# One-layer attention and expert block on one core: fewer rotation-table loads, a later start of the second chunk's projections, one idle product less

## The chip, the cores and the metric

The kernel runs on one core of a Trainium2 chip. The engines of the core that matter here are TensorE (PE in the profile: matrix products, with its weight loads shown apart as PEld), VectorE (DVE), ScalarE (ACT), GpSimd (POOL), and SyncE (SP), which does nothing but issue DMA transfers. ACT and POOL issue some transfers too. The metric is the time of one execution on the device in microseconds (us); of several executions the median is taken.

## The reference

The input x has 2048 rows of 256 numbers. The block is latent attention with rotated positions, then a layer norm, then an expert network, then a second layer norm:

```python
q = (x @ Wq).reshape(B, S, 16, 16)            # 16 heads of 16
c_kv = x @ Wkv_down                           # 64 latent columns
k = (c_kv @ Wk_up)...;  v = (c_kv @ Wv_up)...
q_rope, k_rope = rotated(last 12 of each head, cos, sin)
scores = where(causal, -inf, qf @ kf.T * 0.25)
x = layernorm(x + softmax(scores) @ v)
w, i = top_2_of(softmax(x @ gate_w.T))        # of 16 experts
x = layernorm(x + sum_e w_e * swiglu_e(x) + swiglu_shared(x))
```

All of it is in float32.

## The kernel before, in words

**Chunks, heads, steps.** The 2048 rows are worked on in four chunks `c` of 512. The 16 heads are four groups `g` of four; within a group each head takes 32 partitions: 0 to 15 for its numbers, 16 for a constant, and 20 to 31 for its 12 rotated numbers once more. For each group and chunk of queries the kernel first finds the largest score of each row (`Maxima`: products into four PSUM banks, one a head, then a DVE reduction of each, L515, or L509 on the diagonal, where the mask is added) and later the weighted values (`Weighted`: products, exponentials on ACT, values). Both are cut into steps, listed in `steps`. The dictionary `at` says what else is done at the end of a step: `prologue(c)` turns chunk c of x on PE (eight transposes, tile `pt`, copied to `xT`) and computes its latent columns (tile `pc`, copied to `ckv`); `project_k`, `project_q` and `project_v` compute a group's keys, queries and values of one chunk.

**Order.** PE executes strictly in the order of the program (L142 to L149). All products write to eight PSUM banks taken in turn, so a product waits until the reader of the bank's last content is done. The other engines have their own queues, in an order that the framework chooses.

**The start.** L750 to L756: three idle products (`warm`, 128x512, each two passes on PE as all float32 products are) on constants, then `prologue(0)`, `project_k(0, 0)`, `project_q(0, 0)` and `prologue(1)`. Then come the steps. Steps 0, 1 and 2 are the three diagonal maxima of group 0, chunk 0; steps 3 to 6 the maxima of chunk 1's queries against chunk 0's keys; at step 7 the first weighted products join. `project_k(0, 1)` and `project_q(0, 1)` stand at the end of step 1, `prologue(2)` at the end of step 3, `project_v(0, 0)` at step 4, `project_k(0, 2)` at step 6, `prologue(3)` at step 7.

**Rotation.** `project_k` multiplies the keys' two products `pk` by a cosine and a sine table, `cs[c]` (128 partitions x 2 x 512), and adds the two. For group 0, chunk 0 both multiplications are DVE's (L430, L434); otherwise the second is copied by ACT (L436) and multiplied by POOL (L437). The sum is always POOL's (L439). `project_q` does the same with one table `cq[c]` (128 x 512), on DVE for group 0, chunk 0 (L450), else ACT and POOL (L452, L453). In each 32 partitions of `cs` and `cq` the first 20 come from rows 0 to 19 of the table in DRAM (`rope`, 32 rows x 2 x 2048, rows 17 to 31 zero) and the last 12 from rows 4 to 15: two loads for each of four heads, so eight loads for `cs[c]` and eight for `cq[c]` (`load_rope`, L317 to L326).

**Loads.** SP issues, in this order: chunk 0 of x (L350), `cs[0]`, chunk 1 of x, the value weights `wvs` twice (L361), the tables of chunk 1, chunk 2 of x, its tables, chunk 3 and its tables, the weights of the other groups, the gate, the experts' weights, and a clearing of a buffer in DRAM. ACT's queue issues the latent weights `wkds` (two loads), the key weights `wks[0]` (two loads, one for each 64 partitions), the query weights and `cq[0]`. All of these transfers share eight semaphores: each issue waits until the last transfer of its semaphore has landed. `double(g)` (L339) copies columns of the weights on POOL; it waits for their loads.

Of the kernel before, what the change touches and what calls it, by code (L numbers as in the profile page):

```python
# [13 lines left out]
ALU = mybir.AluOpType  # L14
# [3 lines left out]
P = 128  # L18
S, E = 2048, 256
H, HD, LAT = 16, 16, 64  # L20
NOPE, RD = 4, 12
G = 4
PAD = 32
LOW = HD + NOPE
ONE = HD
CH = 512
# [11 lines left out]


NBLK = 28  # L40
WARM = 3
LAST = 2
OFTEN, SELDOM = 9, 12
DEPTH = 2
# [6 lines left out]
def block_kernel(  # L51
# [14 lines left out]
    nc = tc.nc  # L66
# [8 lines left out]
        out=qmask, in_=qmask, pattern=[[-1, CH]], base=CH - P, channel_multiplier=1,  # L75
# [16 lines left out]
    cs = [const.tile([P, 2, CH], F32, tag=f"cs{c}", name=f"cs{c}") for c in range(3)]  # L92
# [15 lines left out]
        out=before, in_=before, pattern=[[1, P]], base=0, channel_multiplier=-1,  # L108
# [36 lines left out]
    def matmul(*args, **kw):  # L145
        pe(nc.tensor.matmul, *args, **kw)

    def transpose(*args):
        pe(nc.tensor.transpose, *args)  # L149
# [139 lines left out]
    with ExitStack() as att:  # L289
# [11 lines left out]
        wks = [ap1.tile([P, P], F32, tag=f"wks{g}", name=f"wks{g}") for g in range(G)]  # L301
        wvs = ap1.tile([P, G * P], F32, tag="wvs", name="wvs")
# [6 lines left out]
        cq = [ap1.tile([P, CH], F32, tag=f"cq{c}", name=f"cq{c}") for c in range(NCH)]  # L309
        ckv = [ap1.tile([2 * LAT, CH], F32, tag=f"ckv{c}", name=f"ckv{c}") for c in range(NCH)]  # L310
# [4 lines left out]
            )  # L315

        def load_rope(c, queries, queue):  # L317
            of = rope[:, :, c * CH : (c + 1) * CH]
            for j in range(4):
                r = PAD * j  # L320
                if queries:
                    queue.dma_start(out=cq[c][r : r + LOW], in_=of[:LOW, 0, :])
                    queue.dma_start(out=cq[c][r + LOW : r + PAD], in_=of[NOPE:HD, 1, :])
                else:
                    queue.dma_start(out=cs[c][r : r + LOW], in_=of[:LOW])
                    queue.dma_start(out=cs[c][r + LOW : r + PAD], in_=of[NOPE:HD])  # L326

        sines = {}

        def load_weights(g, queue):  # L330

            of = slice(g * P, (g + 1) * P)
            for a in range(2):
                queue.dma_start(out=wks[g][a * LAT : (a + 1) * LAT], in_=wk[:LAT, a, of])
            sines[g] = wkp.tile([P, 2, P], F32, tag="pr", name=f"sines{g}")
            for a, to in enumerate((wqs[g], sines[g])):
                queue.dma_start(out=to, in_=wq[:, a, of].rearrange("(k p) m -> p k m", p=P))

        def double(g):  # L339


            w = wks[g].rearrange("p (h d) -> p h d", d=PAD)
            nc.gpsimd.tensor_copy(w[:, :, LOW:], w[:, :, NOPE:HD])
            for k in range(2):
                w, o = (
                    a[:, k].rearrange("p (h d) -> p h d", d=PAD) for a in (wqs[g], sines[g])
                )
                nc.gpsimd.tensor_copy(w[:, :, LOW:], o[:, :, NOPE:HD])

        load_x(0)  # L350
        for a in range(2):
            nc.scalar.dma_start(
                out=wkds[:, :, a * LAT : (a + 1) * LAT], in_=wkd.rearrange("(k p) l -> p k l", p=P)
            )
        load_weights(0, nc.scalar)
        load_rope(0, False, nc.sync)
        load_x(1)
        load_rope(0, True, nc.scalar)
        double(0)
        for a in range(2):  # L360
            nc.sync.dma_start(out=wvs[a * LAT : (a + 1) * LAT], in_=wv[:LAT])  # L361
        load_rope(1, False, nc.sync)
        load_rope(1, True, nc.sync)
        load_x(2)
# [5 lines left out]
        for g in range(1, G):  # L370
            load_weights(g, nc.sync)
        nc.sync.dma_start(out=gw, in_=gate.rearrange("(k p) n -> p k n", p=P))
        for k in range(2):
            for w, at, o, n in (
# [3 lines left out]
                    out=w13[:, k, :, at : at + n],  # L378
                    in_=w[k * P : (k + 1) * P, :NF].rearrange("p (n f) -> p n f", f=INTER)[
                        :, :, o : o + n  # L380
                    ],
# [11 lines left out]
        for e in range(NEXP):  # L393
            nc.sync.dma_start(
                out=xg[e * S : (e + 1) * S, :].rearrange("(r p) e -> p r e", p=P),
                in_=blank.unsqueeze(1).to_broadcast([P, TT, ROW]),
            )
        nc.sync.dma_start(
            out=xg[NEXP * S :, :], in_=blank
        )  # L400

        qs, ks, vs, qa, pm, avs = {}, {}, {}, {}, {}, {}

        def bank(name):
            return ps_sc.tile([P, CH], F32, tag="sc", name=name)

        def prologue(c):

            copy = nc.scalar.copy if c else nc.vector.tensor_copy
            for k in range(2):  # L410
                pt = bank(f"pt{c}_{k}")
                for t in range(4):
                    transpose(pt[:, t * P : (t + 1) * P], xr[c][:, t, k * P : (k + 1) * P], ident)
                copy(xT[c][:, k, :], pt)
            pc = bank(f"pc{c}")
            for k in range(2):
                matmul(
                    pc, lhsT=wkds[:, k, :], rhs=xT[c][:, k, :], start=(k == 0), stop=(k == 1)
                )
            copy(ckv[c], pc)  # L420

        def project_k(g, c):
            tmp = wk1.tile([P, 2, CH], F32, tag="rot", name=f"rot{g}_{c}")
            pk = [bank(f"pk{g}_{c}_{a}") for a in range(2)]
            for a in range(2):
                r = slice(a * LAT, (a + 1) * LAT)
                matmul(
                    pk[a], lhsT=wks[g][r], rhs=ckv[c][r], start=True, stop=True
                )
            nc.vector.scalar_tensor_tensor(  # L430
                tmp[:, 0, :], pk[0], unit, cs[c][:, 0, :], ALU.add, ALU.mult
            )
            if (g, c) == (0, 0):
                nc.vector.tensor_tensor(tmp[:, 1, :], pk[1], cs[c][:, 1, :], ALU.mult)  # L434
            else:
                nc.scalar.copy(tmp[:, 1, :], pk[1])  # L436
                nc.gpsimd.tensor_tensor(tmp[:, 1, :], tmp[:, 1, :], cs[c][:, 1, :], ALU.mult)  # L437
            ks[g, c] = kv.tile([P, CH], F32, tag="k", name=f"k{g}_{c}")
            nc.gpsimd.tensor_tensor(ks[g, c], tmp[:, 0, :], tmp[:, 1, :], ALU.add)  # L439

        def project_q(g, c):
            pq = bank(f"pq{g}_{c}")
            for k in range(2):
                matmul(
                    pq, lhsT=wqs[g][:, k], rhs=xT[c][:, k, :],
                    start=(k == 0), stop=(k == 1),
                )
            qs[g, c] = wk3.tile([P, CH], F32, tag="q", name=f"q{g}_{c}")
            if (g, c) == (0, 0):
                nc.vector.tensor_tensor(qs[g, c], pq, cq[c], ALU.mult)  # L450
            else:
                nc.scalar.copy(qs[g, c], pq)  # L452
                nc.gpsimd.tensor_tensor(qs[g, c], qs[g, c], cq[c], ALU.mult)  # L453
# [184 lines left out]
        def whole_m(g, c):  # L638
            return [(g, c, t, kc) for t in range(4) for kc in range(c)]
# [31 lines left out]
        m = whole_m(1, 3)  # L671
# [5 lines left out]
        for g in range(1, G):  # L677
# [9 lines left out]
            else:  # L687
                m = whole_m(g + 1, 3)
# [22 lines left out]
        def put(step, what, *args):  # L711
            at.setdefault(step, []).append(lambda: what(*args))

        for step, what, c in (
            (1, project_k, 1), (1, project_q, 1), (3, prologue, 2), (4, project_v, 0),
            (6, project_k, 2), (7, prologue, 3), (9, project_v, 1), (9, project_q, 2),
            (14, project_k, 3), (17, project_q, 3), (19, project_v, 2), (32, project_v, 3),
        ):
            if what is prologue:
                put(step, what, c)  # L720
            else:
                put(step, what, 0, c)
# [27 lines left out]
        warm = bank("warm")  # L750
        for i in range(WARM):
            matmul(warm, lhsT=ones, rhs=qmask, start=True, stop=True)
        prologue(0)
        project_k(0, 0)
        project_q(0, 0)
        prologue(1)  # L756
        prior = None
        step = 0
        while step < len(steps) or prior or at:
            m, s = steps[step] if step < len(steps) else (None, None)  # L760
            m = m and Maxima(*m)
# [31 lines left out]
    for j, r, o in ((0, 0, slice(0, H1)), (1, 0, slice(H1, INTER)), (1, H2, slice(0, H1 - H2))):  # L793
        nc.sync.dma_start(
            out=w2r[r : r + o.stop - o.start, j],
            in_=w2[:NF, :].rearrange("(n q) e -> q n e", q=INTER)[o],
        )
    hidden_rows = [fp1.tile([P, 2, 2 * P], F32, tag=f"hT{i}", name=f"hT{i}") for i in range(3)]
    for a in hidden_rows:
# [16 lines left out]
        out=upto, in_=upto, pattern=[[1, NEXP], [-1, NEXP]], base=0, channel_multiplier=0,  # L816
# [404 lines left out]
```

## Time and profile before

| what | value |
| --- | --- |
| median of 11 executions | 779.58 us (776.95 to 780.95) |
| the profiled execution, its own time | 777.5 us |
| its span from first to last instruction | 775.8 us |
| mean granted clock of TensorE | 0.973 |
| instructions | 14499 |
| DMA | 72.55 MB, mean 94 GB/s |

Three views of the profile are used. The page gives each engine's busy time and share of the span, and the chain of work that ended last: followed back from the last instruction, at each step to whatever released it. The timeline lists groups of instructions with start, length, engine, line, output and inputs, shapes and count; in brackets stands how long the engine had been idle and what ended that. An engine name with a q at its end (SPq, ACTq) is the engine's sequencer, which issues DMAs. The windows give, for a stretch of time, the busy time and count of PE, PEld, DVE, ACT and POOL, then the clock that was granted to TensorE as a share of full speed, the busy share of the DMA engines and their rate.

The clock column shows 1.00 also where there is no record, as in the first microseconds.

### The profile page before, as it was taken

How to read it: one execution, taken by the hardware profiler on the slowest of the kernel's cores; microseconds unless marked ns; L12 is line 12 of the kernel's file. 1: busy time of each engine (PE TensorE's matmuls, PEld its weight loads, DVE VectorE, ACT ScalarE, POOL GpSimd, SP SyncE). 2: the span in 40 equal slices, each digit the busy share in tenths (PEclk: the TensorE clock that was granted, in tenths of full speed). 3: DMA queues.
4: the chain of work that ended last, by engine and by line, in shares of the span. 5: the costliest groups of instructions: out<-in, count | busy, mean ns of one | idle time of the engine just before them, and what ended most of it. 6: DMA issues, size and time to landing. Idle time of an engine off the chain costs nothing.

```text
span 775.8 us, 14499 instructions
## 1 busy us (share of the span) xinstructions
PE 733.4 (95%) x5074; PEld 361.5 (47%) x5074; DVE 524.7 (68%) x1434; ACT 445.0 (57%) x908; POOL 342.0 (44%) x510
## 2 busy tenths in 40 slices
PE   6898999999999999999999999999869989999994
PEld 3343443444334343544334444344234658887542
DVE  2677798887677887778688678897546623332275
ACT  1243647478787787777788778866443112223356
POOL 3241646534467455657454655440725304445300
PEclk9899999999999999999999999999969989999998
DMA  5459999992000000001000000000208233332172
GB/s 150 132 146 258 328 330 327 330 329 87 3 1 1 1 2 1 2 20 38 1 2 2 1 3 1 1 2 1 89 22 213 69 103 108 112 104 65 29 231 98
DMA packets 75981, 72.55 MB, mean 94 GB/s; under 512 B 20890, under 2 KB 70141, under 8 KB 75904
## 3 DMA queue, kind: packets, MB, share of 16 engines
q1 hardware_dynamic: 70936, 62.43, 28.4%
q0 software_dynamic: 3504, 8.43, 3.2%
q10 hardware_dynamic: 1464, 0.72, 0.4%
q8 instruction: 42, 0.69, 0.4%
q14 instruction: 35, 0.29, 0.1%
HBM read 27.09 MB, written 45.65 MB: 94 GB/s over the span
## 4 chain that ended last, share of the span: by engine, by line
PE 80%; DVE 6%; issue 3%; DMA 3%; SPq 2%; ACT 2%; another core or an unknown queue 2%; POOL 1%; ACTq 0%; POOLq 0%; DVEq 0%
PE s L143 22%; PE av L143 17%; PE m L143 14%; PE py L143 4%; PE ab L143 4%; PE pq L143 3%; PE c L143 2%; PE pk L143 2%; PE ph L143 2%; PE pv L143 1%; PE px L143 1%; PE pz L143 1%; DVE pm L515 1%; PE lg L143 1%
## 5 line engine op out<-in xcount | busy, mean ns | idle before, releaser
L571 ACT ACTIVATE p<-s 128x512 f32<-128x512 f32 (+1 forms) x576 | 284.9, 580 | 106.4 <-PE m L143 62.4
L143 PE MATMUL m<-k,q 32*128 32x512 f32 (+3 forms) x1280 | 283.6, 566 | 4.7 <-POOL q L453 4.7
L143 PE MATMUL s<-qa,k 32*128 32x512 f32 (+3 forms) x1280 | 275.7, 560 | 3.6 <-DVE qa L533 2.0
L515 DVE TENSOR_REDUCE pm<-m 128x1 f32<-128x512 f32 x384 | 237.6, 684 | 46.1 <-PE m L143 45.0
L610 POOL TENSOR_TENSOR avs<-avs,more 128x512 f32<-128x512 f32 (+2 forms) x110 | 128.7, 1170 | 129.4 <-ACT more L609 118.8
L143 PEld LDWEIGHTS s<-qa,k 32*128 32x128 f32 x1280 | 110.0, 187 | 118.0 <-ACT p L571 58.6
L143 PE MATMUL av<-p,v 128*32 128x512 f32 (+3 forms) x1280 | 150.5, 546 | 0.6 <-ACT p L571 0.5
L509 DVE CUSTOM_DVE_ANT_0 m<-m,qmask 128x128 f32<-128x128 f32 (+3 forms) x256 | 117.6, 526 | 40.1 <-PE m L143 33.4
L143 PEld LDWEIGHTS m<-k,q 32*128 32x128 f32 x1280 | 112.3, 184 | 35.2 <-issue 9.6
L143 PEld LDWEIGHTS av<-p,v 128*32 128x32 f32 x1280 | 28.1, 108 | 99.5 <-ACT p L571 56.6
L982 POOL DMA_INDIRECT yg<-yb,to x41 | 40.4, 984 | 74.0 <-ACT yb L970 53.1
L580 POOL TENSOR_SCALAR_AFFINE_SELECT p<-p 128x128 f32<-128x128 f32 (+1 forms) x192 | 59.6, 330 | 28.7 <-ACT p L571 26.9
L609 ACT COPY more<-av 128x512 f32<-128x512 f32 (+2 forms) x110 | 60.8, 553 | 19.9 <-PE av L143 14.8
L143 PE MATMUL h<-xT,cs 128*128 128x512 f32 (+1 forms) x96 | 43.3, 597 | 2.3 <-ACT u L836 1.4
L281 POOL DMA_INDIRECT xg<-xr,slot x32 | 31.2, 975 | 21.4 <-issue 15.7
L143 PE MATMUL py<-w2r,hT 112*128 112x256 f32 (+1 forms) x164 | 39.8, 380 | 0.0
L509 DVE DVE_READ_ACCUMULATOR2_ANT pm<- 128x1 f32 x256 | 36.7, 143 | 0.0
L143 PE MATMUL ab<-xT,w 128*112 128x256 f32 x128 | 33.9, 388 | 0.0
L143 PEld LDWEIGHTS py<-w2r,hT 112*128 112x128 f32 x164 | 30.8, 190 | 6.1 <-ACT hT L1021 0.5
L143 PE MATMUL pq<-xT,wqs 128*128 128x512 f32 x64 | 31.7, 618 | 0.0
L437 POOL TENSOR_TENSOR rot<-rot,cs 128x512 f32<-128x512 f32 x15 | 19.1, 1270 | 23.9 <-ACT rot L436 23.9
L143 PEld LDWEIGHTS h<-xT,cs 128*128 128x128 f32 (+1 forms) x96 | 16.9, 181 | 24.1 <-issue 17.4
(166 smaller groups left out, 658.1 us busy)
## 6 DMA issues: line engine op xcount, KB each, us to landing
xg<-hot SPq DMA_DIRECT2D x16, 2064.0 KB
xb<-xg SPq DMA_DIRECT2D x16, 258.0 KB
got<-yg SPq DMA_DIRECT2D x8, 512.0 KB
w<-in_w_dram SPq DMA_DIRECT2D x4, 896.0 KB
xr<-in_x_dram SPq DMA_DIRECT2D x4, 512.0 KB
w<-in_w_dram SPq DMA_DIRECT2D x4, 512.0 KB
out_dram<-o SPq DMA_DIRECT2D x8, 256.0 KB
w2r<-in_w_dram SPq DMA_DIRECT2D x1, 1792.0 KB
```

What stands on the lines that cost most here:

```text
L143: tc.keep_in_program_order(op(*args, **kw))
L281: put = nc.gpsimd.indirect_dma_start(out=xg[:, :], out_offset=bass.IndirectOffsetOnAxis(ap=slot[:, j, i : i + 1], axis=0), in_=xr[c][:, t, ...
L437: nc.gpsimd.tensor_tensor(tmp[:, 1, :], tmp[:, 1, :], cs[c][:, 1, :], ALU.mult)
L509: nc.vector.tensor_tensor_reduce(out=ps[:, of], in0=ps[:, of], in1=qmask[:, CH - (of.stop - of.start) :], scale=1.0, scalar=3.0 * NEG, op0 ...
L515: nc.vector.tensor_reduce(to, ps, AX.X, ALU.max)
L571: nc.scalar.activation(pr[:, :n], ps[:, :n], AF.Exp, scale=SCALE)
L580: nc.gpsimd.affine_select(out=diag, in_=diag, pattern=pattern, base=0, channel_multiplier=-1, compare_op=ALU.is_ge, fill=0.0,)
L609: nc.scalar.copy(more[:, n0:], pv[:, n0:])
L610: nc.gpsimd.tensor_tensor(to, to, more[:, n0:], ALU.add)
L982: nc.gpsimd.indirect_dma_start(out=yg[:, :], out_offset=bass.IndirectOffsetOnAxis(ap=to, axis=0), in_=yb, in_offset=None, bounds_check=2 * ...
```

## The change

The rotation tables in DRAM are used by their first 16 rows alone: 32 partitions are filled by rows 0 to 15 twice. A chunk's key table takes two loads (cosines, sines; 128 partitions, the 16 rows read eight times by a source step of zero) and its query table four (one a head: 16 cosine rows, then 16 sine rows). Two pairs of weight loads become one each. The warm products are two. The first keys' sum goes to DVE. `prologue` is split into `columns` (turning) and `latent`; only chunk 1's `columns` comes ahead of the steps, while its `latent`, `project_k` and `project_q` come at the end of step 0; chunk 2's prologue comes one step earlier, at the end of step 2.

```diff
-WARM = 3
+WARM = 2
...
         def load_rope(c, queries, queue):
-            of = rope[:, :, c * CH : (c + 1) * CH]
-            for j in range(4):
-                r = PAD * j
-                if queries:
-                    queue.dma_start(out=cq[c][r : r + LOW], in_=of[:LOW, 0, :])
-                    queue.dma_start(out=cq[c][r + LOW : r + PAD], in_=of[NOPE:HD, 1, :])
-                else:
-                    queue.dma_start(out=cs[c][r : r + LOW], in_=of[:LOW])
-                    queue.dma_start(out=cs[c][r + LOW : r + PAD], in_=of[NOPE:HD])
+            of = rope[:HD, :, c * CH : (c + 1) * CH]
+            if queries:
+                for j in range(4):
+                    queue.dma_start(
+                        out=cq[c][PAD * j : PAD * (j + 1)], in_=of.rearrange("d a n -> a d n")
+                    )
+            else:
+                for a in range(2):
+                    half = of[:, a].unsqueeze(0)
+                    queue.dma_start(out=cs[c][:, a], in_=half.to_broadcast([8, HD, CH]))
...
-            for a in range(2):
-                queue.dma_start(out=wks[g][a * LAT : (a + 1) * LAT], in_=wk[:LAT, a, of])
+            queue.dma_start(out=wks[g], in_=wk[:LAT, :, of].rearrange("l a m -> a l m"))
...
-        for a in range(2):
-            nc.sync.dma_start(out=wvs[a * LAT : (a + 1) * LAT], in_=wv[:LAT])
+        nc.sync.dma_start(
+            out=wvs, in_=wv[:LAT].unsqueeze(0).to_broadcast([2, LAT, G * P])
+        )
...
-        def prologue(c):
-
-            copy = nc.scalar.copy if c else nc.vector.tensor_copy
+        def mover(c):
+
+            return nc.scalar.copy if c else nc.vector.tensor_copy
+
+        def columns(c):
+
+            copy = mover(c)
             for k in range(2):
...
+        def latent(c):
             pc = bank(f"pc{c}")
...
-            copy(ckv[c], pc)
+            mover(c)(ckv[c], pc)
+
+        def prologue(c):
+            columns(c)
+            latent(c)
...
-            nc.gpsimd.tensor_tensor(ks[g, c], tmp[:, 0, :], tmp[:, 1, :], ALU.add)
+            adder = nc.gpsimd if g or c else nc.vector
+            adder.tensor_tensor(ks[g, c], tmp[:, 0, :], tmp[:, 1, :], ALU.add)
...
-            (1, project_k, 1), (1, project_q, 1), (3, prologue, 2), (4, project_v, 0),
+            (0, latent, 1), (0, project_k, 1), (0, project_q, 1), (2, prologue, 2),
+            (4, project_v, 0),
             (6, project_k, 2), (7, prologue, 3), (9, project_v, 1), (9, project_q, 2),
...
-        prologue(1)
+        columns(1)
```

More of the change, by code (lines that the diff above doesn't have):

```diff
@@ L718, in block_kernel @@
         ):
-            if what is prologue:
+            if what in (prologue, latent):
                 put(step, what, c)
```

## The prediction

> **What bounds the kernel now.** I read the page first, for the engines and the chain of work that ended last.
>
> ```profile
> PE 733.4 (95%) x5074; PEld 361.5 (47%) x5074; DVE 524.7 (68%) x1434; ACT 445.0 (57%) x908; POOL 342.0 (44%) x510
> ...
> PE 80%; DVE 6%; issue 3%; DMA 3%; SPq 2%; ACT 2%; another core or an unknown queue 2%; POOL 1%; ACTq 0%; POOLq 0%; DVEq 0%
> ```
>
> TensorE (PE) is busy 95% of the span and makes 80% of the chain. Work taken from another engine in mid-kernel would give nothing; but the DMA and SP shares of the chain (5%) must sit where PE has nothing to do, and all three edits lie in the first 45 us. So I went to the timeline of that stretch (start, length, engine, line; in brackets the engine's idle time and what ended it).
>
> ```profile
> 2.88 4.53 PE L143 MATMUL warm<-qmask,ones 128*128 128x512 f32 x6 [2.88 <-POOL ones L112]
> ...
> 12.09 0.51 SPq L313 DMA_DIRECT2D xr<-in_x_dram  x1
> ...
> 14.14 0.75 DVE L430 SCALAR_TENSOR_TENSOR rot<-pk,unit,cs 128x512 f32<-128x512 f32 x1 [2.80 <-DMA cs<-in_rope_dram]
> ...
> 16.40 1.88 PE L143 MATMUL pt<-ident,xr 128*128 128x128 f32 x8 [1.92 <-DMA xr<-in_x_dram]
> ...
> 18.10 2.89 PE L143 MATMUL pc<-xT,wkds 128*128 128x512 f32 x4
> ...
> 20.91 1.79 PE L143 MATMUL m<-k,q 32*128 32x512 f32 x16
> ...
> 30.13 2.08 PE L143 MATMUL m<-k,q 32*128 32x512 f32 x8 [2.69 <-POOL q L453]
> ...
> 37.00 2.48 DVE L515 TENSOR_REDUCE pm<-m 128x1 f32<-128x512 f32 x4 [2.31 <-PE m L143]
> ```
>
> Three stalls stand here. DVE waits 2.80 us for the first rotation table (14.14). PE waits 1.92 us for the second chunk of x (16.40), which SP issued only at 12.09, behind eight table loads. And though the first queries were ready at 16.08 and the first keys at 16.84, the first maxima wait until 20.91, because PE runs in program order and chunk 1's turning and latent product stand ahead. A fourth follows: q of chunk 1 comes late (PE idle 2.69 us to 30.13). From 37 us DVE is nearly always busy, until the rotation of chunk 2's keys at 44.78, my last mark. The windows give clock and DMA load (after the engines: granted clock, DMA share, GB/s).
>
> ```profile
> 14.00:16.00 2.00, 0.48 (x2) 0.00 (x0) 1.86 (x3) 0.00 (x0) 0.43 (x1) 1.00 0.99 334
> ...
> 17.00:19.00 2.00, 2.00 (x7) 1.38 (x7) 0.00 (x0) 1.17 (x2) 0.00 (x0) 0.50 0.28 81
> ```
>
> After the 1.9 us gap the clock is halved, so the work ahead of the first maxima is slow as well. And the DMA engines moved 334 GB/s where a large load was queued, 72 to 130 elsewhere before 30 us: the loads are bound by their issues and waits, not by bytes.
>
> **The change, part by part.** I lay the first 38 us out anew from measured lengths; times after the change are in italics.
>
> *Warm products.* One idle product less is two passes. Passes start 0.85 us apart (weight loads at 3.89, 4.74, 5.59). x's first chunk is there at 5.32, when SP's wait for it ends. The turning so starts at *6.3*, not 7.24: 0.9 us. Everything to the first queries' products follows at its old distances: latent product *7.7*, ckv *9.8* to *10.4* on DVE, keys' products *10.5*, queries' products *11.55* to *13.55* (before: 12.49 to 14.47).
>
> *Table loads.* For chunk 0, SP issues two loads instead of eight. Eight cost 6.5 us of issue (1.01 and seven of about 0.78) besides waits: each DMA takes one of eight semaphores and waits for its last user. The new form (128 rows of 2 KB, 16 source rows read eight times) is not in the trace. Nearest rows: 0.45 to 0.51 us for x's 512 rows, 0.59 for 64 rows of wvs, 1.01 for the dearest table issue; bounds 0.3 and 1.0, I take 0.6. Bytes stay alike. x's load (512 KB) took 4.3 us from issue to landing (12.09 to 16.39), a table part 3.0 (6.60 to 9.6). Both halves of the table should land by *8* to *9*, wanted at *11.2*. The next load of x must wait for a semaphore, the first of which returns near 5: issue *5.5* to *6.5*, landing *10.5* to *11.5*, wanted at *13.55*. If it takes up to 2 us more, it costs nothing; beyond, 1 us for 1 us. On ACT the query table's four loads replace eight (0.29 to 0.61 each), landing about *10*, wanted at *13.6*. Merging wks and wvs takes one issue from each queue (0.5 to 0.8) and is hidden. For chunks 1 to 3 SP saves 6 x 0.78 + 4 x 0.33 = 6 us each, so its later loads run well ahead: hidden, nothing counted.
>
> *First keys on DVE.* Rotation *11.2* to *12.6* (0.75 and 0.68), then the sum on DVE, which I price by DVE's 128x512 row, 0.68, against 1.27 on POOL (bounds 0.5 and 1.3): keys at *13.3*. Queries: product done *13.55*, DVE 0.68, ready *14.3*. DVE has nothing else; even 1.3 would stay hidden.
>
> *The move.* Ahead of the first maxima PE has only chunk 1's turning, eight transposes: 1.04 us at full clock (1.88 at half). *13.55* to *14.6*; the maxima start at **14.65 instead of 20.91: 6.3 us**. Their four reductions (2.6 us) run *15.8* to *18.4*. Behind them PE has the latent product (2.0 us, *15.7* to *17.65*), the ACT copy (*18.3*), keys (1.07), queries (1.98 to *21.4*); then the other two diagonal steps, *21.4* to *23.1*. These now come after the projections where one came before, so DVE, which ran without a break from 22.07 to 30.08, is idle some 3 us in between: its diagonal work ends at *26.9* instead of 30.08, only 3.2 us earlier. What decides next is q of chunk 1: ACT copies the keys' second half by *20.3*, POOL does its multiply, sum and query multiply (1.27 each): *24.1* instead of 30.08, hidden behind chunk 2's prologue, which the change puts ahead of the first whole maxima: turning *23.1*, latent product until *26.4* (ACT copies among it). The maxima of chunk 1 start at *26.4*, their reductions at *27.5*. From there DVE sets the pace, and its next step need not wait for a prologue in between: *30.0* for the step that began at 37.00. Then 2.48, 0.6 for qa, 4.87 for two steps: the rotation of chunk 2's keys begins at *38.0*, against 44.78. **Sum: 6.8 to 7.0 us; I take 6.9.**
>
> What comes after is the same list in the same order with the same PSUM buffers, bound by DVE and PE in turn, so a shift passes through. POOL's copies of the later weights, which waited on DMA (4.2 us of waits, 48 to 54), may come free; no PE wait hangs on them, 0 to 0.3 us.
>
> The profiled execution took 777.5 us (span 775.8), so it would take 770.6. The median of the runs is 779.58, 2.1 above it, and the gain does not depend on which: **772.7**.
>
> [...] Full-rate passes begin 0.43 us apart (13.03, 13.46), warm ones 0.85, and the change comes at 6.38, after 3.5 us of idle products. [...]
>
> **Rivals.**
> *B, the clock rises late.* If two warm products don't raise it, the turning (1.04 to 1.88) and four latent passes (0.36 us more each) run at half: 2.2 us of the gain go. [...] Against: the turning follows at once and PE stays busy. 779.6 - 4.7 = **774.9**.
> *C, DVE gives back the front.* If the stretch is bound by the diagonal's end (3.2 us earlier) and the prologue's return saves nothing, **776.4**. For: DVE idles between the first two diagonal steps. Against: in the present trace it idles 1.9 and 2.3 us before the next two steps anyway, and both go.
> *D, the loads come no sooner.* If x's second chunk still lands near 18, its turning at half clock ends at 19.9: 1 us gained, **778.6**. Against: 334 GB/s in 14 to 16 us, and only some ten DMAs stand before it.
> *E, slower: repeated reads of one row get in each other's way.* Place: the table loads, 256 packets a chunk, 16 for each of 16 DMA engines. Now a 2 KB packet takes 0.084 us in the trace. Chunk 1's table is wanted at *19.1* and lies behind 4.9 + 16p + 2.2 (x, wvs) + 16p + 1.2: above p = 0.34 it is late, above 0.55 the whole gain is gone, and at 0.7 the time is about **784**. For: no such load is in the trace. Against: wvs reads 64 rows twice without harm.
> *F, more.* If the second half-clock stretch (30 to 33) and the third (67 to 71) go as well, 2 to 3 us more: **770.0**.
>
> **How the numbers follow.** Forecast 0.60, B 0.15, C 0.08, F 0.05: together 0.88 for faster by over 0.2% (1.6 us, about what a measurement of this kernel can tell from no change). D 0.06: within. E 0.06: slower. The range 769.5 to 776.5 takes in the forecast with 1 us either way for the unknown prices and 1 for the median, B, C and F but for a margin: leaving out D and E, 0.12, and some of the edges.
>
> **What would show it.** Right: turning at 6.3; no DVE wait for cs near 11; x's second load issued by 7 and no PE wait before 13.6; first maxima at 14.65; no half clock before 25; chunk 1's first whole maxima at 26.4; chunk 2's key rotation at 38.0. Each step that fails moves the later ones by the same amount. The forecast is wrong if the rotation of chunk 2's keys is early but PE's later steps are not: then something after 45 us, which I take to be a plain shift, has a date of its own.

## The result

The changed kernel is slower: median **809.66 us** (807.69 to 814.39, 12 executions) against 778.96 us of the kernel before in the same session (46 executions); ratio **1.040** (1.0383 to 1.0416). The forecast was 772.7. The profiled execution took 809.75 us, its span is 808.0 against 775.8, its mean granted clock 0.954 against 0.973. The page of the changed kernel, busy times and chain:

```profile
PE 736.3 (91%) x5072; PEld 361.0 (45%) x5072; DVE 525.5 (65%) x1435; ACT 445.6 (55%) x908; POOL 341.5 (42%) x509
...
PE 76%; DVE 7%; DMA 6%; issue 3%; SPq 2%; ACT 2%; another core or an unknown queue 1%; POOL 1%; ACTq 0%; POOLq 0%; DVEq 0%
```

No engine but PE is busier by more than 1 us. PE has one idle product less and is still busy 2.9 us longer (736.3 us against 733.4), at a lower mean clock. The rest of the 32 us are waits, and the DMA share of the chain has doubled (3% to 6%). The timeline of PE in the changed kernel shows where:

```profile
6.46 1.22 PE L143 MATMUL pt<-ident,xr 128*128 128x128 f32 x8
...
12.84 1.33 PE L143 MATMUL pk<-ckv,wks 64*128 64x512 f32 x4 [2.84 <-POOL wks L345]
14.83 3.78 PE L143 MATMUL pq<-xT,wqs 128*128 128x512 f32 x4 [0.66 <-POOL wqs L350]
...
22.26 1.14 PE L143 MATMUL m<-k,q 32*128 32x512 f32 x8 [1.93 <-DVE q L464]
...
65.70 3.79 PE L143 MATMUL m<-k,q 32*128 32x512 f32 x16 [24.41 <-POOL q L467]
```

The first maxima come at 22.26, where the forecast had 14.65 and the kernel before 20.91; chunk 1's first whole maxima at 65.70 instead of 30.13, after 24.41 us in which PE had nothing. What they wait for is `q` of chunk 1, on POOL. POOL's timeline in the changed kernel:

```profile
14.99 0.53 POOL L533 MEMSET nm<- 128x512 f32 x1
55.47 0.22 POOL L345 COPY wks<-wks 128x48 f32<-128x48 f32 x1 [39.94 <-DMA wks<-in_wk_dram]
...
61.47 0.39 POOL L350 COPY wqs<-sines 128x48 f32<-128x48 f32 x2 [0.84 <-DMA sines<-in_wq_dram]
61.83 1.26 POOL L450 TENSOR_TENSOR rot<-rot,cs 128x512 f32<-128x512 f32 x1
63.16 1.26 POOL L453 TENSOR_TENSOR k<-rot 128x512 f32<-128x512 f32 x1
64.38 1.26 POOL L467 TENSOR_TENSOR q<-q,cq 128x512 f32<-128x512 f32 x1
```

This is the main finding. POOL sits idle for 39.94 us, until the key weights of the *next* group of heads have landed, copies the weights of groups 1 to 3 (L345, L350), and only then does chunk 1's rotation. Before the change the same three operations came first, and the copies after them:

```profile
25.41 1.27 POOL L437 TENSOR_TENSOR rot<-rot,cs 128x512 f32<-128x512 f32 x1 [8.58 <-ACT rot L436]
27.59 1.26 POOL L439 TENSOR_TENSOR k<-rot 128x512 f32<-128x512 f32 x1 [0.91 <-DVE rot L430]
28.81 1.27 POOL L453 TENSOR_TENSOR q<-q,cq 128x512 f32<-128x512 f32 x1
...
46.88 0.22 POOL L343 COPY wks<-wks 128x48 f32<-128x48 f32 x1
```

Nobody wrote this order: the copies stand at the end of the same step of the program (step 5) in both kernels, but the framework now puts them ahead.

A smaller, second loss stands before it. The first queries were delayed by their table, as DVE's timeline shows (its last two rows are used further down):

```profile
21.51 0.69 DVE L464 TENSOR_TENSOR q<-pq,cq 128x512 f32<-128x512 f32 x1 [5.24 <-DMA cq<-in_rope_dram]
...
67.80 4.88 DVE L529 TENSOR_REDUCE pm<-m 128x1 f32<-128x512 f32 x8 [31.52 <-PE m L143]
...
77.97 0.75 DVE L443 SCALAR_TENSOR_TENSOR rot<-pk,unit,cs 128x512 f32<-128x512 f32 x1
```

`cq` was to land near 10 and landed at 21.5. In the DMA view of the stretch 14 to 26 us (40 slices of 0.3 us; busy tenths of the 16 DMA engines, then GB/s) the rate has a floor:

```profile
DMA  1111113545412555521111111111111111111111
GB/s 51 48 48 48 55 48 150 198 178 198 137 55 109 191 184 164 184 75 48 55 41 55 48 48 55 48 48 48 48 55 48 48 55 48 48 55 48 48 55 48
```

A 2 KB packet takes 0.084 us here, 24 GB/s for one DMA engine, so 48 GB/s is *two* engines at work and fourteen idle (DMA share 0.13 of sixteen from 22 to 26 us), although loads are queued. The start and length of each packet in the trace say the same: from 19.7 to 20.6 us, 11 packets of ACT's queue and 12 of SP's take turns, and for nearly all of that time two are in flight. No record names an engine, but as the packets follow one another in two rows and both queues alternate in each, loads from both queues share the same two.

The last mark, the rotation of chunk 2's keys, comes at 77.97 instead of 44.78: 33.2 us late, against 32.2 in the span. After it little more is gained or lost.

### The profile page after: what moved, and what is told of

Read it like the earlier page. It is cut to its first block, busy times and chain, and to the rows that moved or that the text cites. A ratio compares the mean times of both kernels' runs of the same rounds, so it can differ in the third digit from the quotient of the medians.

```text
span 808.0 us, 14414 instructions
## 1 busy us (share of the span) xinstructions
PE 736.3 (91%) x5072; PEld 361.0 (45%) x5072; DVE 525.5 (65%) x1435; ACT 445.6 (55%) x908; POOL 341.5 (42%) x509
## 4 chain that ended last, share of the span: by engine, by line
PE 76%; DVE 7%; DMA 6%; issue 3%; SPq 2%; ACT 2%; another core or an unknown queue 1%; POOL 1%; ACTq 0%; POOLq 0%; DVEq 0%
PE s L143 22%; PE av L143 16%; PE m L143 14%; PE py L143 4%; PE ab L143 4%; PE pq L143 3%; DMA sines<-in_wq_dram 2%; PE c L143 2%; PE pk L143 2%; PE ph L143 2%; DMA cq<-in_rope_dram 1%; DMA xr<-in_x_dram 1%; PE pv L143 1%; PE px L143 1%
## 5 line engine op out<-in xcount | busy, mean ns | idle before, releaser
L143 PE MATMUL m<-k,q 32*128 32x512 f32 (+3 forms) x1280 | 281.9, 566 | 28.4 <-POOL q L467 26.4
L143 PE MATMUL pq<-xT,wqs 128*128 128x512 f32 x64 | 33.5, 649 | 0.7 <-POOL wqs L350 0.7
L143 PEld LDWEIGHTS h<-xT,cs 128*128 128x128 f32 (+1 forms) x96 | 16.9, 181 | 24.1 <-issue 17.4
L482 ACT COPY v<-pv 128x256 f32<-128x256 f32 x32 | 10.4, 380 | 29.2 <-PE pv L143 28.9
```

What stands on the lines that cost most here:

```text
L143: tc.keep_in_program_order(op(*args, **kw))
L482: nc.scalar.copy(v.rearrange("p (b a m) -> p b a m", a=2, m=P)[:, :, a, :], pv[a][:, : 2 * P].rearrange("p (b m) -> p b m", m=P),)
```

## The experiments

Two theories. **T1, the queue:** the loss is POOL's order; POOL waits in line for weights that nobody needs yet. **T2, the loads:** a merged load is slow by itself, because it is carried by few DMA engines, and everything behind it is late. A third, the forecast's rival E (repeated reads of a row slow each other), competes with T2. The experiments ran on chips on which the kernel before took 765.6 to 765.9 us, so differences are compared, not times. The expectations of pin, old_loads, new_loads_only and tables_pin give times for a kernel before of 779 us, as in the result above.

| kernel | median us | minus before | ratio (95%) | first maxima | chunk 1's whole maxima | chunk 2's keys |
| --- | --- | --- | --- | --- | --- | --- |
| forecast | | -6.9 | | 14.65 | 26.4 | 38.0 |
| before | | 0 | | 20.91 | 30.13 | 44.78 |
| changed | 809.66 | +30.7 | 1.0400 (1.0383 to 1.0416) | 22.26 | 65.70 | 77.97 |
| pin | 769.79 | +4.2 | 1.0057 (1.0036 to 1.0078) | 21.95 | 41.11 | 52.44 |
| old_loads | 766.67 | +1.1 | 1.0004 (0.9980 to 1.0028) | 18.39 | 33.04 | 44.38 |
| new_loads_only | 798.72 | +33.1 | 1.0422 (1.0375 to 1.0469) | 21.84 | 64.67 | 79.34 |
| before_copies_first | 792.14 | +26.3 | 1.0335 (1.0308 to 1.0362) | 19.56 | 56.96 | 71.95 |
| rope_new_w_old_pin | 767.23 | +1.4 | 1.0017 (0.9989 to 1.0044) | 23.23 | 37.66 | 48.99 |
| rope_old_w_new_pin | 770.89 | +5.1 | 1.0061 (1.0030 to 1.0091) | 18.70 | 36.59 | 47.92 |
| before_tables_pin | 762.82 | -3.0 | 0.9954 (0.9925 to 0.9983) | 18.46 | 27.67 | 42.15 |
| tables | 762.28 | -3.5 | 0.9946 (0.9924 to 0.9969) | 15.17 | 31.02 | 43.30 |
| **tables_pin** | **757.50** | **-8.1** | **0.9895 (0.9856 to 0.9933)** | 14.22 | 25.91 | 37.24 |
| tables_pin_again | 758.88 | -7.0 | 0.9907 (0.9884 to 0.9930) | 14.80 | 26.49 | 37.82 |
| tables_pin_warm3 | 760.61 | -5.3 | 0.9931 (0.9911 to 0.9951) | 16.49 | 28.17 | 39.50 |

The three last columns are starts in one execution, the profiled one. It is not always near the median: of pin (774.61 us), tables (766.46), before_tables_pin (766.80) and rope_new_w_old_pin (770.04) it is the slowest one measured. A start also varies by itself. Up to their first maxima, before and before_copies_first do the same work, and yet they differ by 1.35 us there; chunk 1's turning took 1.88 us in the one and 1.09 in the other.

**pin: POOL's order held.** The changed kernel, with its loads, but the copies of groups 1 to 3 kept behind chunk 1's rotation:

```diff
-            nc.gpsimd.tensor_copy(w[:, :, LOW:], w[:, :, NOPE:HD])
+            held = tc.keep_in_program_order if g else (lambda op: op)
+            held(nc.gpsimd.tensor_copy(w[:, :, LOW:], w[:, :, NOPE:HD]))
...
-                nc.gpsimd.tensor_tensor(qs[g, c], qs[g, c], cq[c], ALU.mult)
+                held = (lambda op: op) if g else tc.keep_in_program_order
+                held(nc.gpsimd.tensor_tensor(qs[g, c], qs[g, c], cq[c], ALU.mult))
...
-            put(5, double, g)
+            put(11, double, g)
```

> The changed kernel with one thing undone: POOL is held to the order of before, in which the copies of the later groups' weights come behind the rotations of chunks 1 and 2. Loads, warm products and the move stay. Queue theory (the copies stand ahead of the rotations on POOL and wait there for weights that land near 60 us): the wait of 24.4 us ahead of the first whole maxima goes; they start at about 41 instead of 65.7 us, and the time is 784 to 787, still 5 to 8 above before because the loads land late. Load theory (the merged loads are slow, and everything waits for tables and x; the order on POOL hides nothing of its own): the first whole maxima stay later than 55 us and the time stays above 799.

Measured +4.2 us instead of +30.7 (5 to 8 were expected). T1 holds: 26.5 us of the loss are the queue. What is left is no gain but a loss, and PE now waits for data in two places: 2.08 us at 21.95 for DVE's `q`, which waited 5.78 us for `cq`, and 5.31 us at 35.63 for the third chunk of x.

```profile
21.95 1.14 PE L143 MATMUL m<-k,q 32*128 32x512 f32 x8 [2.08 <-DVE q L466]
...
35.63 1.94 PE L143 MATMUL pt<-ident,xr 128*128 128x128 f32 x8 [5.31 <-DMA xr<-in_x_dram]
```

**old_loads: all of the change but its loads.** Sixteen table loads a chunk and the weights in two loads each, as before; the move, the sum on DVE and two warm products stay. The framework now puts the rotations first of itself.

> The changed kernel with the loads of before (16 a chunk, two for wks, two for wvs); two warm products, the first keys' sum on DVE and the move stay; POOL's order is left to the framework, which now puts the rotations first again. If the merged loads are the whole loss, directly or through POOL's order: no wait for the copies, the first maxima near 18.4 instead of 20.9 (x's second chunk lands at 16.4 as before), the first whole maxima near 31, and a time of 776.5 to 778.5, a gain of 1 to 3. If the move of the projections itself costs something: at or above 780.

Measured +1.1 us (no difference shown): the gain of 1 to 3 us that was expected does not come. PE and DVE show why:

```profile
16.49 1.97 PE L143 MATMUL pt<-ident,xr 128*128 128x128 f32 x8 [3.15 <-DMA xr<-in_x_dram]
18.39 2.09 PE L143 MATMUL m<-k,q 32*128 32x512 f32 x8
```

```profile
28.27 0.57 DVE L520 CUSTOM_DVE_ANT_0 m<-m,qmask 128x384 f32<-128x384 f32 x1 [5.07 <-PE m L143]
```

The queries' products end at 13.3, the second chunk of x lands at 16.49, and after the gap the eight transposes run at half clock (1.97 us, not 1.04; granted clock 0.50 from 16.4 to 20.4 us). The first maxima still come 2.5 us earlier than before, but DVE then has nothing for 5.07 us, in which PE does the projections that now stand between the diagonal steps. Chunk 1's whole maxima start at 33.04 instead of 30.13. So the forecast's rival D (x comes late) is seen here together with its rival C (DVE gives back the front): PE's new order is worth nothing while x comes late.

**new_loads_only: the loads alone.** The kernel before with the merged loads and nothing else.

> The kernel before with the merged loads alone: three warm products, the first sum on POOL, the old places of the projections. POOL's order is left to the framework, which puts the weights' copies ahead of chunk 1's rotations, as in the changed kernel. If loads and POOL's order are the whole loss: the same wait, the first whole maxima near 66 us, but chunk 2's prologue behind them: 809 to 815. If the loss needs the move of the projections: below 795.

Measured +33.1 us: the whole loss. Its POOL timeline has the same gap and the same copies ahead of the rotation:

```profile
54.45 0.22 POOL L345 COPY wks<-wks 128x48 f32<-128x48 f32 x1 [38.51 <-DMA wks<-in_wk_dram]
```

So the move, the sum and the idle product have no part in the loss; the loads have two, their own slowness and the order that comes with them.

**before_copies_first: the order alone.** The kernel before, old loads, old program, but the copies held ahead of chunk 1's rotation (`put(0, double, g)` for `put(5, ...)`, with the same holds as in pin).

> The kernel before, all loads and places as they were, with one thing changed: POOL is held to an order in which the copies of the later groups' weights come ahead of chunk 1's rotations. Queue theory (the order alone makes the loss, whatever the loads): the last copies wait until about 54 as before, the three POOL steps end at 57.9 instead of 30.1, and the time is 26 to 29 above the kernel before. If the order costs only in company with the late merged loads: less than 10 above.

```profile
46.63 0.22 POOL L344 COPY wks<-wks 128x48 f32<-128x48 f32 x1 [29.99 <-DMA wks<-in_wk_dram]
...
53.09 1.26 POOL L439 TENSOR_TENSOR rot<-rot,cs 128x512 f32<-128x512 f32 x1
...
55.64 1.26 POOL L456 TENSOR_TENSOR q<-q,cq 128x512 f32<-128x512 f32 x1
```

POOL's timeline of this kernel is that of the changed kernel over again: the rotation begins at 53.09, where in the kernel before it began at 25.41. Measured +26.3 us, with no load changed: T1's mechanism is shown by itself (26 to 29 were expected), and its size agrees with what pin gave back (26.5).

**rope_new_w_old_pin and rope_old_w_new_pin: which loads are slow.** POOL's order held in both; the first merges only the tables' loads, the second only the weights'.

> The changed kernel with POOL's order held and wks and wvs in two loads each as before; the merged table loads stay (two for cs with the 16 rows read eight times, four for cq). If the merged weight loads (outermost count 2, so few DMA engines) were what held up the start: keys' and queries' products of chunk 0 near 10.4 and 11.5, first maxima near 15, 3 to 7 below the kernel before. If the table loads are what is slow: first maxima after 19, at or above the kernel before.

> The mirror of it: POOL's order held, 16 table loads a chunk as before, wks and wvs merged into one load each. If the merged weight loads hold up the start: keys' product near 12.2, queries' near 14.4, first maxima at 18.5 or later, 0 to 4 above the kernel before. If the table loads are what is slow: as the changed kernel with all old loads, within 1 of the kernel before, keys' product near 10.4.

```profile
22.48 0.69 DVE L466 TENSOR_TENSOR q<-pq,cq 128x512 f32<-128x512 f32 x1 [7.75 <-DMA cq<-in_rope_dram]
```

```profile
17.67 1.09 PE L143 MATMUL pt<-ident,xr 128*128 128x128 f32 x8 [3.33 <-DMA xr<-in_x_dram]
...
32.08 1.47 PE L143 MATMUL pt<-ident,xr 128*128 128x128 f32 x8 [3.37 <-DMA xr<-in_x_dram]
```

The first line is DVE of the kernel with merged tables, the others PE of the kernel with merged weights. With merged tables the first queries wait 7.75 us for `cq`, and the first maxima come at 23.23, later than in pin; it is `cq` that is slow. With merged weights the keys' product does not wait for its weights (11.30); two later waits for x make 6.7 us, and the time is +5.1, more than either branch of the expectation had. old_loads has the first of these waits too (3.15 us). The second comes from SP's waits in the first 40 us:

```profile
SPq L326 <- DMA wvs<-in_wv_dram: 3.4, 1, 3.4
```

The merged `wvs` was issued at 14.06. The eighth issue after it stood 3.4 us for it, until 23.83, and the third chunk of x behind was issued at 27.80, where old_loads has 23.56. A load on few engines thus holds up its queue as well as its own reader.

Beside old_loads (+1.1, the same order on POOL), merged weights cost 4.0 us, and merged tables 0.3, which isn't told from nothing: they are no worse than the sixteen small loads that they replace, but 9.5 us worse than the plain form of tables_pin (below). The two costs don't add up: pin, with both, is at +4.2.

**load_shapes: the loads by themselves.** tables_pin (below) with seven loads, into a tile that nobody reads, at a time when no other DMA runs (DMA share 0.00 from 204 to 209 us). Each writes the same tile, so each waits for the one before (only the two halves go together), and the distance from issue to issue is a load's duration. It is one execution.

```diff
+            plain = nc.sync.dma_start(out=scratch, in_=rope[:, 0, n])
+            eight = nc.sync.dma_start(
+                out=scratch, in_=rope[:HD, 0, n].unsqueeze(0).to_broadcast([8, HD, CH])
+            )
+            two = nc.sync.dma_start(
+                out=scratch, in_=wv[:LAT].unsqueeze(0).to_broadcast([2, LAT, G * P])
+            )
+            each = nc.sync.dma_start(
+                out=scratch[:, : 2 * P].rearrange("p (a m) -> p a m", a=2)[:, 0],
+                in_=wk[:LAT, :, :P].rearrange("l a m -> a l m"),
+            )
+            for a in range(2):
+                nc.sync.dma_start(out=scratch[a * LAT : (a + 1) * LAT], in_=wv[:LAT])
+            nc.sync.dma_start(out=scratch, in_=rope[:, 0, n])
```

> The version with tables in DRAM and POOL's held order, plus seven loads into a tile that nothing reads, one after the other (each but the sixth waits for the landing of the one before), placed where the DMA engines are otherwise idle: 256 KB of 128 plain rows; 256 KB as 16 rows read eight times (the new cs form); 256 KB as 64 rows read twice (the new wvs form); 64 KB as two halves of 64 rows of 512 bytes (the new wks form, no row read twice); 128 KB of 64 rows, twice at once (the old wvs form); the first again. From issue to the next issue. Engine theory (a load is spread over as many DMA engines as its outermost count, 16 at most; a 2 KB packet takes 0.084 us on one engine, and some 2.6 us are fixed): 3.3, 3.9, 8.0, 4.3, 3.4 for the pair; DMA share about 0.13 while the third runs. Repetition theory (rows read several times get in each other's way): the second is the slowest, the fourth as fast as plain rows.

SP's timeline, and the windows between the issues (the last two columns: busy share of the 16 DMA engines, GB/s):

```profile
209.54 0.35 SPq L765 DMA_DIRECT2D scratch<-in_rope_dram  x1
212.32 0.73 SPq L766 DMA_DIRECT2D scratch<-in_rope_dram  x1
216.49 0.55 SPq L769 DMA_DIRECT2D scratch<-in_wv_dram  x1
224.05 0.51 SPq L772 DMA_DIRECT2D scratch<-in_wk_dram  x1
227.43 1.15 SPq L777 DMA_DIRECT2D scratch<-in_wv_dram  x2
230.88 0.35 SPq L778 DMA_DIRECT2D scratch<-in_rope_dram  x1
```

```profile
209.50:212.30 2.80, 2.80 (x28) 1.60 (x28) 1.64 (x4) 1.74 (x5) 1.97 (x4) 1.00 0.31 94
212.30:216.50 4.20, 4.20 (x36) 1.51 (x36) 3.60 (x8) 3.56 (x9) 2.01 (x2) 1.00 0.18 64
216.50:224.00 7.50, 7.50 (x68) 2.90 (x66) 5.77 (x14) 6.39 (x14) 5.06 (x9) 1.00 0.11 37
```

The first three loads bring the same 256 KB in 128 rows of 2 KB. 128 plain rows take 2.8 us, 16 rows read eight times 4.2, 64 rows read twice 7.6. Length times share times 16 gives the work in microseconds of one DMA engine (engine-us): 13.9, 12.1 and 13.2, the same within a sixth. So no packet got dearer; the work was spread over fewer engines. The packets' own starts and lengths count them: the plain load has up to 16 in flight at once, the second seldom more than eight, the third two for 4.4 of the 5.8 us in which it moves data. 128 packets of 0.084 us are 10.8 engine-us: 0.7 us on sixteen engines, 1.3 on eight, 5.4 on two, so 0.7 and 4.7 more than the plain form; measured 1.4 and 4.8 more. Of the eightfold load's 1.4, some 0.5 is a later first packet (1.46 us after the issue, the plain load's 1.00), which the count of engines doesn't explain. Rival E's theory falls: it would have the eightfold repetition dearest, and the twofold one is. The last forms fit as well: the merged key weights, a quarter of the bytes, take 3.4 us (4.3 were expected), as long as the whole 256 KB in two plain halves (3.5). The 64 KB in a plain form were not timed.

Three outermost counts (the size of the slowest dimension) were so timed: 128, 8 and 2, with up to 16, about eight and two packets in flight. What engine theory says of other counts is not shown, and neither are its 2.6 us as a fixed part: 2.8, 4.2 and 7.6 us less 0.7, 1.3 and 5.4 leave 2.1, 2.9 and 2.2. The form of `cq`, whose outermost count is two as well, was not timed here, but the changed kernel shows it on two engines: from 14.0 to 15.5 us 35 packets of 2 KB of ACT's queue, all of `cq[0]`, were started, with two in flight. For `wks` the same is the author's estimate.

With two engines for all of them, `wks`, `wvs` and the tables `cq` of chunks 0 and 1 (832 KB) at 48 GB/s make 17 to 18 us end to end. They fall in the stretch from the first one's issue (1.93) to 26 us, where the floor still stands, and share it with x and `cs`.

**tables_pin: few loads that use all engines.** What the forecast had priced, in another way: the tables lie in DRAM as the tiles want them (128 rows of cosines, sines and the query table), so a chunk takes two plain loads; the weights take two loads each as before; POOL's order is held.

```diff
-                for j in range(4):
-                    queue.dma_start(
-                        out=cq[c][PAD * j : PAD * (j + 1)], in_=of.rearrange("d a n -> a d n")
-                    )
+                queue.dma_start(out=cq[c], in_=rope[:, 2, at_])
...
-                for a in range(2):
-                    half = of[:, a].unsqueeze(0)
-                    queue.dma_start(out=cs[c][:, a], in_=half.to_broadcast([8, HD, CH]))
+                queue.dma_start(out=cs[c], in_=rope[:, :2, at_])
...
-    return t
+    r = np.concatenate([t[:HD]] * 8)
+    q = np.concatenate([t[:HD, 0], t[:HD, 1]] * 4)
+    return np.concatenate([r, q[:, None]], axis=1)
```

> The changed kernel with tables that lie in DRAM as they are wanted (128 rows: cosines, sines, query table), so that a chunk takes two loads of 128 plain rows, like x; wks and wvs in two loads each as before; POOL held to the order of before. If the forecast failed only by the loads' shape and POOL's order: the first maxima near 14.7, the first whole maxima near 26.4, chunk 2's key rotation near 38, 771 to 774.5. If few large loads are late whatever their shape: the first maxima not before 18 and 776 or more.

Its PE timeline is the forecast's timetable:

```profile
6.17 1.04 PE L143 MATMUL pt<-ident,xr 128*128 128x128 f32 x8
7.55 1.98 PE L143 MATMUL pc<-xT,wkds 128*128 128x512 f32 x4 [0.35 <-DVE xT L415]
10.36 1.13 PE L143 MATMUL pk<-ckv,wks 64*128 64x512 f32 x4 [0.83 <-issue]
11.42 1.99 PE L143 MATMUL pq<-xT,wqs 128*128 128x512 f32 x4
13.24 1.04 PE L143 MATMUL pt<-ident,xr 128*128 128x128 f32 x8
14.22 1.14 PE L143 MATMUL m<-k,q 32*128 32x512 f32 x8
...
25.91 2.00 PE L143 MATMUL m<-k,q 32*128 32x512 f32 x16
```

The forecast had 6.3, 7.7, 10.5, 11.55, 13.55, 14.65 and 26.4 for these rows; each comes 0.1 to 0.5 us earlier, and the keys of chunk 2 0.8 us (37.24 against 38.0). 8.1 us below the kernel before, and the fastest kernel of the study.

**tables, before_tables_pin, tables_pin_again, tables_pin_warm3: the parts.** tables is tables_pin with POOL's order left to the framework; before_tables_pin has the new tables and the held order in the program of before (three idle products, old places, sum on POOL); tables_pin_warm3 is tables_pin with three idle products, beside tables_pin run again.

> Two loads a chunk from tables laid out in DRAM, as in the kernel that has them and POOL's held order, but POOL's order left to the framework, which puts the copies of the later weights ahead of chunk 1's rotations. In the held kernel those weights have landed by about 25. Queue theory (the price of the order is the landing of the last weights, less the time at which the rotations could have run): copies until 25.8, the three POOL steps until 29.6, the first whole maxima at 29.6 instead of 25.9, so 3.7 above the held kernel and about 4 below the kernel before. If the order on POOL costs nothing where loads are fast: as the held kernel, 8 below.

> The kernel before with the tables laid out in DRAM (two loads a chunk) and POOL's order held; three warm products, the first sum on POOL and the old places of the projections. It tells what the move, the warm product and the sum are worth once the loads are early. By the forecast's steps: first maxima near 17.8 behind chunk 1's latent product, its q near 27, chunk 2's key rotation near 40.6 against 37.2 with the move: 4 below the kernel before, 3 to 4 above the version with all edits. If the loads are the whole gain: as that version, 8 below.

> The version with tables laid out in DRAM, two loads a chunk, wks and wvs as before, POOL's order held, all other edits: once more, for its interval and beside the version with three warm products. 7 to 9 below the kernel before.

> The same with three warm products. By the forecast's step the third product holds up all that follows by 0.9: 0.9 above the version with two. If two products sometimes leave the first projections at the half clock (rival B), the two differ less, by 0 to 0.5, or three are faster.

In tables the framework again puts the copies first; their weights have landed by 27 us there, so PE's wait for `q` is 4.10 us, not 24.41:

```profile
31.02 3.79 PE L143 MATMUL m<-k,q 32*128 32x512 f32 x16 [4.10 <-POOL q L460]
```

What the order costs is set by when the loads land. Early loads in the old program are worth 3.0 us, and the move with two idle products and the sum on DVE another 4 to 5 on top, though alone (old_loads) it gave nothing. The third idle product delays the turning by 1.7 us (8.16 against 6.45) and the medians differ by 1.7; their intervals overlap, so the time alone would not show it (the two profiled executions even stand the other way, 757.18 with three and 760.85 with two). The expectation had 0.9.

## Why the prediction was wrong

**What failed: "POOL's copies of the later weights ... may come free; no PE wait hangs on them, 0 to 0.3 us".** That holds only while the copies stand behind chunk 1's rotation on POOL, and the prediction took this order from the trace of before as if it were the program's. Nothing wrote it. With the rotation behind them, chunk 1's maxima hang on the weights of three groups: 26.3 us, shown by before_copies_first. That q of chunk 1 is ready at "24.1" failed with it: it was ready at 65.6.

**What failed: "The new form ... I take 0.6" and "cq landing about 10".** The issue's price was within its bounds: 1.48 us for the two of `cs[0]`, 0.74 each. But a load was priced by its issue and its bytes, and landing dates were carried over from rows of plain loads ("a table part 3.0"). How many DMA engines carry a load went with its form. The prediction's own words for this step stand in its rival E, "16 for each of 16 DMA engines": all sixteen were taken to carry the new forms, where load_shapes shows about eight for the form of `cs` and two for that of `wvs` (up to 16 for plain rows), and the floor of 48 GB/s in the changed kernel two while `cq` was queued. `cq[0]` landed at 21.5, the first weights at 12.56 instead of in time for 10.5, and ACT's four issues of `cq[0]` stretched to 8.79 us. "Merging wks and wvs ... is hidden" fell for the same reason. The cost is the distance from pin to tables_pin, 12.3 us (11.2 by its second run).

Both terms together account for the miss: from the forecast to the result are 37.6 us (from -6.9 to +30.7), the order makes 26.3 to 26.5 and the loads 11.2 to 12.3. The 26.5 and the 12.3 are steps of one chain (changed, pin, tables_pin), so their sum is its length in any case; the 26.3 of before_copies_first is a measurement apart from it.

**What held.** *Warm products:* turning at 6.46 (forecast 6.3). Its worth was mis-sized, 0.9 against 1.7, because six idle passes kept 0.85 us apart to the end in tables_pin_warm3 (5.49 us, where the trace of before has 4.53). Rival B's late clock does occur: in tables the turning takes 1.91 us instead of 1.04, and the first maxima come 0.95 us later than in tables_pin. *x's second load* was issued at 5.53, as forecast. *The sum on DVE* took 0.69 (0.68). *The move:* each length and the order of PE's rows were right, and in tables_pin so were the dates; the gain was 7.0 to 8.1 (6.9), with loads of another form than the forecast had and POOL's order held. It needs early loads as its condition, which the prediction named (rival D) and old_loads shows. *After 45 us a plain shift:* 33.2 us late at the last mark, 32.2 at the end.

**The rivals.** E had the right side and the wrong mechanism: in load_shapes the work stayed at 12.1 to 13.9 engine-us, repeated or not. It looked for the price in the packet, where the engines' number was the price. The rates that the prediction itself quoted, 334 GB/s for a plain load, should have been asked of every new form: how many of the sixteen will carry it?

**Open.** Why the framework changes POOL's order isn't shown. The copies come first in the changed kernel, new_loads_only and tables, behind in before and old_loads; so fewer table loads are enough to turn it, in both forms tried. What it weighs is in no trace. No run holds POOL's order in the kernel before, which has it anyway; that the hold itself costs nothing is taken for granted. What the half clock (granted 0.50 from 14 to 20 us) adds to the changed kernel's late start is not told apart from its late loads.

## What to carry to other kernels

Price a DMA by how it is laid over the DMA engines, not by issues and bytes alone: two plain loads of 64 rows each took 3.5 us together in load_shapes, one merged load of the same rows, outermost count two, 7.6. An order that no line of the program sets may not outlast the next change; where a long wait stands on a queue, hold what must come ahead of it, or the two may turn around, as here. And a step that is moved forward is worth only what its inputs' landing dates allow.

## What the runs showed of the hardware

The same 256 KB in 128 rows took 2.8, 4.2 or 7.6 us alone on idle queues by the form of the access pattern alone. Plain table loads in a row kept the engines busy: in tables_pin the windows show 315 GB/s from 6 to 8 us (DMA share 1.15) and 324 from 9 to 14 (1.05), where the changed kernel had 186 and 112. A load on few engines also held up the queue behind it, through the semaphore that it keeps: 3.4 us for `wvs` in rope_old_w_new_pin. And the clock after two idle products is not the same in every execution (turning in 1.04, 1.22, 1.34 or 1.91 us); in six executions each, no gain of a third product is seen that would pay for the 1.7 us that it takes; with three, the turning took 1.06 us in before_tables_pin and 1.31 in tables_pin_warm3.
